# First layer of a two-layer selective-scan network: states in pairs, softplus passes in other slots, old y added at the copy, z copied on VectorE

## The chip, the cores and the metric

One core of a Trainium2 chip runs the whole program. The metric is the device time of one execution in microseconds. Four runs of the kernel before took 11094.7 to 11108.07 us, median 11100.91.

## The reference

Two layers, each with a residual connection, work on x of shape (4, 64, 64, 192). The change touches only the first. In it every image of the batch (4 of them, L = 4096 positions, 192 channels) is normalised and projected to xin and z (384 channels each), and xin is scanned in four directions: by rows, by columns, and both backwards. Cut to what matters:

```python
xz = jnp.einsum('bhwc,ec->bhwe', x, in_proj_weight)
xin, z = jnp.split(xz, 2, axis=-1)
...
delta = jax.nn.softplus(delta + delta_bias[None, :, None])
def step(h, inp):                       # one position of one direction
    dt, ut, bt, ct = inp
    dA = jnp.exp(dt[..., None] * A_k[None])
    dBu = dt[..., None] * bt[:, :, None, :] * ut[..., None]
    h = dA * h + dBu                    # 384 channels x 16 states
    y = jnp.einsum('bkdn,bkn->bkd', h, ct)
    return (h, y)
...
y = out_y[:, 0] + inv_y[:, 0] + wh_y + invwh_y      # the four directions, plus u * D
y = layernorm(y) * jax.nn.silu(z)
return jnp.einsum('bhwd,cd->bhwc', y, out_proj_weight)
```

The sums over the 16 states and over the four directions are what the change is about: y is collected in memory, and each direction adds to what the ones before it have left there.

## The kernel before

`FirstLayer.run` takes the four images one after the other. Between two images, `between` finishes one (normalisation, gate, output projection) and projects the next; then `scans` (L572) does the four directions. Nearly all the time is in `scans`, and within it the order of the work on TensorE, ScalarE, VectorE and GpSimd is the order in which the code issues it (`manual_schedule`); the DMAs all go through SP's queue, in order.

The work of one image is cut into 32 *items*: a direction k (0 to 3) and a chunk c of 512 positions. Items 0 to 15 are directions 0 and 2 (rows, forward and backward), items 16 to 31 directions 1 and 3 (columns), in pairs that run towards each other. An item has 16 *states*, so an image has 512 steps g, and the loop over g is software-pipelined by hand. The 384 channels are three groups d of 128. For state n of an item the engines do the following:

- ScalarE, `b_product` two steps ahead (L716): x in turned form, position on partitions, as delta times u times B of this state, four pieces of 128 positions. `decay` one step ahead (L728): a = exp(A delta), three groups.
- TensorE, `turn_x` one step ahead (L733): transposes of x back to channels on partitions, into PSUM, three buffers, four transposes for each d.
- VectorE, `scan` (L741): the recurrence, one instruction for each d; then a reduce (L751) that copies the last column of h, the `carry` for the next chunk of this direction.
- GpSimd, `c_product` (L755): h times C, in place, after the reduce. Here it is called a product, and c4 is that of state 4.
- TensorE, `add_y` (L768): transposes of h that accumulate in three PSUM banks yp, three steps later (`LAG = 3`); states 0 and 1 are added together at step 4, once the banks are free again.

h is held in seven buffers of one state each (`p7`), a in three, C (`bct`, loaded for two states at once at even steps) in three.

Ahead of the states, `start_y` (L762) puts the old y of the chunk into the banks by an identity matmul, at steps 3 and 4. `load("yold")` gets it from memory: at step 5 of the item before, or, where the direction changes between rows and columns, only after the last item has stored its part (`end_y` at step 3). `end_y` (L781) copies the three banks to SBUF at steps 2 and 3 of the next item, on VectorE, and stores them.

Around this, `Item.steps` (L685) spreads the preparation of the following items over the steps: a tuple (ahead, n, engine, f) runs f at state n of the item that lies `ahead` items before. Delta is a softplus built of passes: dt rows by a matmul (`dt_rows`, L632), `absolute` and `exp` on ScalarE, `plus` (L645) and `minus` (L649) on GpSimd two items ahead, `log` on ScalarE, `rest` (L655) and `total` (L658) on GpSimd one item ahead at states 1 and 4, the dt rows once more, and `delta` (L661) on VectorE at states 7 to 9. `turn` (L675) and `times_u` (L681) follow at states 10 to 13. At each step GpSimd takes the product of the state first and then what `prepare(g, "pool")` has for it.

The gate z is made during items 0 to 8: `gate_in` (L519 by way of `in_proj`) into PSUM at states 13 to 15, `gate_out` (L794) on ScalarE two steps later. The dt rows, the turns of dt, turn_b and the gate share two PSUM buffers (`psm`).

Of the kernel before, what the change touches and what calls it, by code (L numbers as in the profile page):

```python
# [402 lines left out]
class FirstLayer:  # L403
# [168 lines left out]
    def scans(self):  # L572
        nc, tc = self.tc.nc, self.tc
        with ExitStack() as ctx:
            pool = lambda name, bufs, **k: ctx.enter_context(tc.tile_pool(name=name, bufs=bufs, **k))
            p1, p2, p3, p7 = pool("b1", 1), pool("b2", 2), pool("b3", 3), pool("b7", 7)
# [27 lines left out]
            class Item:  # L604
# [80 lines left out]
                def steps(self):  # L685
# [6 lines left out]
                    r += [(2, 15, "pool", self.minus), (1, 2, "act", self.log)]  # L692
                    r += [(1, 1, "pool", self.rest), (1, 4, "pool", self.total)]
# [16 lines left out]
            carry, xTs, xs, as_, hs, cs = {}, {}, {}, {}, {}, {}  # L710
# [26 lines left out]
            def scan(g, d):  # L737
                it, n = flat[g]
                if d == 0:
                    hs[g] = p7.tile([128, ND, LC], F32, name="h")  # L740
# [4 lines left out]
                    0.0 if it.first else carry[it.k, n][:, d : d + 1],  # L745
# [3 lines left out]
                if d == ND - 1:  # L749
                    kept = carry[it.k, n] = pk.tile([128, ND], F32, name=f"carry{it.k // 2}_{n}")  # L750
                    nc.vector.tensor_reduce(kept, last(hs[g], it.k), mybir.AxisListType.X, ALU.max)  # L751
# [5 lines left out]
            def start_y(it, b):  # L757

                if b == 0:
                    it.yp = [ps_y.tile([128, LC], F32, name=f"yp{i}") for i in range(ND)]  # L760
                yo = it.yold.rearrange("p j e -> p (j e)")[:, b * LC : (b + 1) * LC]
                nc.tensor.matmul(it.yp[b], ident, yo, start=True, stop=False, skip_group_check=True)  # L762

            def add_y(g, b):
                it, n = flat[g]
                for i in range(NJ):
# [5 lines left out]
                        start=False,  # L772
# [5 lines left out]
            def end_y(it, b):  # L778
                if b == 0:
                    it.yt = p1.tile([128, NJ, DI], F32, name="yt")  # L780
                nc.vector.tensor_copy(it.yt.rearrange("p j e -> p (j e)")[:, b * LC : (b + 1) * LC], it.yp[b])  # L781
# [9 lines left out]
            def gate_out(t, e):  # L791
                if e == 0:
                    zs[t] = p1.tile([128, ND, LC], F32, name="zg")
                nc.scalar.activation(zs[t][:, e, :], zs.pop((t, e)), AF.Identity, bias=self.bias[:, ND + e : ND + e + 1])  # L794
# [3 lines left out]
            with tc.manual_schedule(engines={nc.tensor.engine, nc.scalar.engine, nc.vector.engine, nc.gpsimd.engine}):  # L798
# [8 lines left out]
                for t in range(NCH):  # L807
                    for e in range(ND):
                        plan.setdefault(t * NS + 13 + e, []).append(("pe", lambda t=t, e=e: gate_in(t, e)))
                        plan.setdefault(t * NS + 15 + e, []).append(("act", lambda t=t, e=e: gate_out(t, e)))  # L810
# [6 lines left out]
                items[0].yold = load("yold", self.y_dram, items[0].k, items[0].c)  # L817
# [8 lines left out]
                for g in range(N + LAG + 1):  # L826
# [11 lines left out]
                    if it is not None:  # L838
# [794 lines left out]
```

## Time and profile before

| | us | share of span |
|---|---|---|
| median of four runs | 11100.91 | |
| the profiled execution | 11094.67 | |
| its span | 11092.5 | 100% |
| scans of image 0, first scan to last | 184.5 to 2377.0 | |
| from the last scan of an image to the first of the next | some 230 | |
| an item in mid-run, first scan to first scan | some 68 | |
| item 16 (rows to columns) | some 86 | |
| VectorE busy | 9690.0 | 87% |
| ScalarE busy | 9776.6 | 88% |
| TensorE busy (matmul) | 9542.3 | 86% |
| GpSimd busy | 8588.4 | 77% |

The granted TensorE clock was 0.939 over the span. A line of groups names the source line, engine, operation, tiles and shape with its count, then busy time, mean nanoseconds of one, and the idle time of the engine in front of it with what ended it. A line of the timeline gives start, length, engine, line, operation, tiles and how many were merged, and in brackets the idle time before it. TensorE's weight loads (PEld) are listed apart from its matmuls. Other groups that the text speaks of:

```
L728 ACT ACTIVATE a<-dt,A_log_f 128x512 f32<-128x512 f32 x6144 | 3978.1, 716 | 0.0
L762 PE MATMUL yp<-yold,ident 128*128 128x512 f32 x768 | 440.6, 658 | 71.5 <-DMA yold<-y 71.5
L661 DVE SCALAR_TENSOR_TENSOR dt<-dp,e 128x512 f32<-128x512 f32 x384 | 255.4, 666 | 65.1 <-POOL e L658 58.5
L781 DVE COPY yt<-yp 128x512 f32<-128x512 f32 x384 | 258.3, 674 | 17.7 <-PE yp L768 17.4 <-issue 0.3
L794 ACT ACTIVATE zg<-zp,bias 128x512 f32<-128x512 f32 x96 | 65.3, 681 | 5.1 <-PE zp L519 5.1
```

### The profile page before, as it was taken

The page shows a single profiled execution, that of the slowest core. Times are in us where ns is not written, and L with a number is a line of the kernel's source. Part 1 is how long each engine was busy: PE and PEld are TensorE (multiplying, and loading weights), DVE is VectorE, ACT ScalarE, POOL GpSimd, SP SyncE. Part 2 cuts the span into 40 slices and gives each one's busy share as a digit, 9 for nine tenths or more (in the row PEclk, how much of TensorE's full clock was granted, in tenths as well). Part 3 has the DMA queues.
Part 4 walks back from the last instruction along what each step waited for, and adds up shares of the span by engine and source line. Part 5 has one row for each costly group of instructions (what it writes and reads, how often), then busy time and mean ns, then how long its engine had stood idle before and what let it go on. Part 6 is the DMA issues. An engine that isn't in the chain of part 4 may idle for free. (4 is left out here: it accounts for less than half of the span.)

```text
span 11092.5 us, 172135 instructions
## 1 busy us (share of the span) xinstructions
PE 9542.3 (86%) x61449; PEld 7262.8 (65%) x61449; DVE 9690.0 (87%) x11515; ACT 9776.6 (88%) x16979; POOL 8588.4 (77%) x2776
## 2 busy tenths in 40 slices
PE   7998888888998888888988888889988888788677
PEld 4776666666776666656766666657766666655366
DVE  4999899976999899968999899949998999878675
ACT  5999999977999999969999999959999999856477
POOL 3999899956999899938999899929998999700270
PEclk8999999998999999998999999989999999989688
DMA  4343344444343344443433444454333434433458
GB/s 125 111 110 99 91 102 98 99 141 126 108 107 99 93 100 98 99 161 109 110 103 95 98 99 97 95 169 109 109 97 96 98 99 98 119 117 122 158 130 275
DMA packets 833672, 1267.54 MB, mean 114 GB/s; under 512 B 102027, under 2 KB 517656, under 8 KB 832293
## 3 DMA queue, kind: packets, MB, share of 16 engines
q1 hardware_dynamic: 827940, 1250.15, 41.5%
q0 software_dynamic: 4864, 6.29, 0.4%
q8 instruction: 488, 8.00, 0.3%
q14 instruction: 380, 3.10, 0.1%
HBM read 955.83 MB, written 300.42 MB: 113 GB/s over the span
## 5 line engine op out<-in xcount | busy, mean ns | idle before, releaser
L755 POOL TENSOR_TENSOR h<-h,bct 128x1536 f32<-128x1536 f32 x2048 | 7065.5, 3473 | 571.9 <-DVE carry L751 471.8
L741 DVE TENSOR_TENSOR_SCAN h<-a,carry,x 128x512 f32<-128x512 f32 x5376 | 6603.2, 1266 | 227.8 <-PE x L733 191.1
L733 PE MATMUL x<-ident,xT 128*128 128x128 f32 x24576 | 3994.3, 286 | 815.3 <-DVE h L741 713.4
L716 ACT ACTIVATE xT<-dtuT,bT 128x384 f32<-128x384 f32 x8192 | 4359.2, 609 | 92.8 <-PE x L733 88.0
L733 PEld LDWEIGHTS x<-ident,xT 128*128 128x128 f32 x24576 | 2797.8, 144 | 2139.4 <-DVE h L741 922.6
L728 ACT ACTIVATE a<-dt,A_log_f 128x512 f32<-128x512 f32 x6144 | 3978.1, 716 | 0.0
L768 PE MATMUL yp<-ident,h 128*128 128x128 f32 x24576 | 3700.9, 277 | 9.2 <-POOL h L755 9.2
L768 PEld LDWEIGHTS yp<-ident,h 128*128 128x128 f32 x24576 | 2942.6, 144 | 78.5 <-issue 62.9
L632 PE MATMUL dp<-xd,w_dtb_f 13*128 13x512 f32 x1536 | 882.8, 657 | 218.5 <-DVE dt L661 214.1
L741 DVE TENSOR_TENSOR_SCAN h<-a,x 128x512 f32<-128x512 f32 x768 | 898.9, 1207 | 190.3 <-PE x L733 114.6
L645 POOL TENSOR_SCALAR wl<-e 128x1536 f32<-128x1536 f32 x128 | 189.6, 1481 | 794.8 <-ACT e L641 404.9
L519 PE MATMUL pp<-xT,w_in 96*128 96x512 f32 x1152 | 537.5, 615 | 1.1 <-DVE xw L562 1.1
L632 PEld LDWEIGHTS dp<-xd,w_dtb_f 13*128 13x128 f32 x1536 | 235.6, 190 | 459.3 <-DVE dt L661 343.4
L762 PE MATMUL yp<-yold,ident 128*128 128x512 f32 x768 | 440.6, 658 | 71.5 <-DMA yold<-y 71.5
L1137 DVE SCALAR_TENSOR_TENSOR acc<-pad,conv_w_s,acc 128x2048 f32<-128x2048 f32 x192 | 439.3, 2342 | 52.4 <-ACT acc L1135 51.8
L638 ACT ACTIVATE e<-dp 128x512 f32<-128x512 f32 x384 | 225.1, 586 | 264.9 <-DVE dt L661 148.9
L1118 POOL MEMSET pad<- 128x66 f32 x12 | 1.9, 160 | 581.8 <-DVE acc L1137 494.3
L658 POOL TENSOR_TENSOR e<-e,wl 128x1536 f32<-128x1536 f32 x128 | 445.5, 3480 | 0.3
L655 POOL TENSOR_TENSOR e<-e,dt 128x1536 f32<-128x1536 f32 x128 | 443.2, 3463 | 0.3
L751 DVE TENSOR_REDUCE carry<-h 128x3 f32<-128x3 f32 x2048 | 322.6, 158 | 70.4
L519 PEld LDWEIGHTS pp<-xT,w_in 96*128 96x128 f32 x1152 | 220.6, 198 | 243.1 <-issue 232.8
L661 DVE SCALAR_TENSOR_TENSOR dt<-dp,e 128x512 f32<-128x512 f32 x384 | 255.4, 666 | 65.1 <-POOL e L658 58.5
(170 smaller groups left out, 6874.5 us busy)
## 6 DMA issues: line engine op xcount, KB each, us to landing
bct<-xp SPq DMA_DIRECT2D x1024, 512.0 KB, 5.1
uT<-uT SPq DMA_DIRECT2D x64, 768.0 KB, 4.7
yold<-y SPq DMA_DIRECT2D x64, 768.0 KB, 7.9
y<-yt SPq DMA_DIRECT2D x64, 768.0 KB, 4.7
uT<-uT SPq DMA_DIRECT2D x128, 384.0 KB, 5.1
yold<-y SPq DMA_DIRECT2D x128, 384.0 KB, 5.5
y<-yt SPq DMA_DIRECT2D x128, 384.0 KB, 4.6
zg<-gate SPq DMA_DIRECT2D x64, 768.0 KB, 6.2
```

The lines of the kernel that those rows point to most:

```text
L519: self.tc.nc.tensor.matmul(pp, self.w_in[:, i, e * 128 : (e + 1) * 128], self.xT[:, i, t * LC : (t + 1) * LC], start=(i == 0), stop=(i == ...
L632: nc.tensor.matmul(self.dp[d], w, self.xd[0 : DR + 1, :], start=True, stop=True)
L655: nc.gpsimd.tensor_tensor(self.e, self.e, self.dt, ALU.subtract)
L658: nc.gpsimd.tensor_tensor(self.e, self.e, self.wl, ALU.add)
L716: nc.scalar.mul(xTs[g][:, j, :], it.dtuT[:, j * DI : (j + 1) * DI], it.bT[:, j, n : n + 1])
L728: nc.scalar.activation(as_[g][:, d, :], it.dt[:, d, :], AF.Exp, scale=scale)
L733: nc.tensor.transpose(xs[g, d][:, j * 128 : (j + 1) * 128], xTs[g][:, j, d * 128 : (d + 1) * 128], ident)
L741: nc.vector.tensor_tensor_scan(along(hs[g][:, d, :], it.k), along(as_[g][:, d, :], it.k), along(xs.pop((g, d)), it.k), 0.0 if it.first els ...
L755: nc.gpsimd.tensor_tensor(hs[g], hs[g], bc(cs[g - n % 2][:, n % 2, :], 1, ND), ALU.mult)
L762: nc.tensor.matmul(it.yp[b], ident, yo, start=True, stop=False, skip_group_check=True)
L768: nc.tensor.matmul(it.yp[b][:, i * 128 : (i + 1) * 128], hs[g][:, d, j * 128 : (j + 1) * 128], ident, start=False, stop=n == NS - 1, is_tr ...
L1137: nc.vector.scalar_tensor_tensor(acc, part(tap), weight(tap), acc, ALU.mult, ALU.add)
```

## The change

Four things in `scans`. h is held in pairs of states (three buffers of two), one reduce serves a pair, the carry is kept by pairs, and the two products of a pair are issued together after the second state. Two of GpSimd's softplus passes change their slot: `minus` from state 15 to 14, `rest` from state 1 to 2, so that at even states, where no product is issued, they stand ahead of the next pair. `start_y` goes: the first add of an item starts the banks, the old y is loaded at step 8 of the item itself, and `end_y` adds it where it copied before. `gate_out` runs on VectorE instead of ScalarE.

```diff
-            p1, p2, p3, p7 = pool("b1", 1), pool("b2", 2), pool("b3", 3), pool("b7", 7)
+            p1, p2, p3 = pool("b1", 1), pool("b2", 2), pool("b3", 3)
...
-                    r += [(2, 15, "pool", self.minus), (1, 2, "act", self.log)]
-                    r += [(1, 1, "pool", self.rest), (1, 4, "pool", self.total)]
+                    r += [(2, 14, "pool", self.minus), (1, 2, "act", self.log)]
+                    r += [(1, 2, "pool", self.rest), (1, 4, "pool", self.total)]
...
-                if d == 0:
-                    hs[g] = p7.tile([128, ND, LC], F32, name="h")
+                if d == 0 and n % 2 == 0:
+                    both[g] = p3.tile([128, 2, ND, LC], F32, name="h")
+                    hs[g], hs[g + 1] = both[g][:, 0], both[g][:, 1]
...
-                    0.0 if it.first else carry[it.k, n][:, d : d + 1],
+                    0.0 if it.first else carry[it.k, n - n % 2][:, n % 2, d : d + 1],
...
-                if d == ND - 1:
-                    kept = carry[it.k, n] = pk.tile([128, ND], F32, name=f"carry{it.k // 2}_{n}")
-                    nc.vector.tensor_reduce(kept, last(hs[g], it.k), mybir.AxisListType.X, ALU.max)
+                if d == ND - 1 and n % 2:
+                    kept = carry[it.k, n - 1] = pk.tile([128, 2, ND], F32, name=f"carry{it.k // 2}_{n}")
+                    nc.vector.tensor_reduce(kept, last(both.pop(g - 1), it.k), mybir.AxisListType.X, ALU.max)
...
-            def start_y(it, b):
-
-                if b == 0:
-                    it.yp = [ps_y.tile([128, LC], F32, name=f"yp{i}") for i in range(ND)]
-                yo = it.yold.rearrange("p j e -> p (j e)")[:, b * LC : (b + 1) * LC]
-                nc.tensor.matmul(it.yp[b], ident, yo, start=True, stop=False, skip_group_check=True)
-
             def add_y(g, b):
                 it, n = flat[g]
+                if n == 0 and b == 0:
+                    it.yp = [ps_y.tile([128, LC], F32, name=f"yp{i}") for i in range(ND)]
...
-                        start=False,
+                        start=n == 0 and i == 0,
...
-                nc.vector.tensor_copy(it.yt.rearrange("p j e -> p (j e)")[:, b * LC : (b + 1) * LC], it.yp[b])
+                part = slice(b * LC, (b + 1) * LC)
+                yt, yo = (t.rearrange("p j e -> p (j e)")[:, part] for t in (it.yt, it.yold))
+                nc.vector.tensor_add(yt, it.yp[b], yo)
...
-                nc.scalar.activation(zs[t][:, e, :], zs.pop((t, e)), AF.Identity, bias=self.bias[:, ND + e : ND + e + 1])
+                nc.vector.tensor_scalar(zs[t][:, e, :], zs.pop((t, e)), self.bias[:, ND + e : ND + e + 1], None, ALU.add)
...
-                items[0].yold = load("yold", self.y_dram, items[0].k, items[0].c)
...
-                            if (n, d) == (LAG, 1) and it is not None and it.yold is None:
-                                it.yold = load("yold", self.y_dram, it.k, it.c)
...
-                        c_product(g)
+                        if n % 2:
+                            c_product(g - 1)
+                            c_product(g)
                         late.append(g)
                         prepare(g, "pool")
-                        if n == 5 and i + 1 < len(items) and items[i + 1].k % 2 == it.k % 2:
-                            q = items[i + 1]
-                            q.yold = load("yold", self.y_dram, q.k, q.c)
+                        if n == 8:
+                            it.yold = load("yold", self.y_dram, it.k, it.c)
```

The order of the adds is unchanged: `late` and `ready` still release a state three steps after its scan.

## The prediction

> **What bounds the kernel now.** I read the page first, then the timelines of VectorE, GpSimd and TensorE over one work item, then the waits, then the change of direction and the end of a batch. "State" n is 0 to 15 within an item; c4 is the product of state 4.
>
> ```profile
> PE 9542.3 (86%) x61449; PEld 7262.8 (65%) x61449; DVE 9690.0 (87%) x11515; ACT 9776.6 (88%) x16979; POOL 8588.4 (77%) x2776
> L755 POOL TENSOR_TENSOR h<-h,bct 128x1536 f32<-128x1536 f32 x2048 | 7065.5, 3473 | 571.9 <-DVE carry L751 471.8
> L741 DVE TENSOR_TENSOR_SCAN h<-a,carry,x 128x512 f32<-128x512 f32 x5376 | 6603.2, 1266 | 227.8 <-PE x L733 191.1
> L751 DVE TENSOR_REDUCE carry<-h 128x3 f32<-128x3 f32 x2048 | 322.6, 158 | 70.4
> ```
>
> Four engines at 77 to 88% over the span are a warning: inside the scans everything is nearly full, so the order of work decides. VectorE is nearest to the bound:
>
> ```profile
> 1004.71 3.62 DVE L741 TENSOR_TENSOR_SCAN h<-a,carry,x 128x512 f32<-128x512 f32 x3
> 1008.37 0.16 DVE L751 TENSOR_REDUCE carry<-h 128x3 f32<-128x3 f32 x1
> 1019.68 0.66 DVE L781 COPY yt<-yp 128x512 f32<-128x512 f32 x1
> 1020.26 1.27 DVE L741 TENSOR_TENSOR_SCAN h<-a,carry,x 128x512 f32<-128x512 f32 x1
> 1047.66 3.62 DVE L741 TENSOR_TENSOR_SCAN h<-a,carry,x 128x512 f32<-128x512 f32 x3 [1.03 <-PE x L733]
> ```
>
> Three scans back to back and their reduce make 3.77 us a state (1004.71 to 1008.48); a copy costs 0.58 (1019.68 to 1020.26). An item takes 68.1 us (mean of the 20 items a batch that I call late: 9 to 15 and 18 to 30). I cut it at two scan starts: A runs from scan (14,0) of the item before to scan (8,1), mean 41.46; B from there to scan (14,0), mean 26.64. In A VectorE hardly idles; the item's 2.1 us of idling lie in B, at states 9 to 11, and end mostly with a turn of x (L733): TensorE stands at a dt row until a PSUM buffer is freed.
>
> GpSimd is late already, in streaks:
>
> ```profile
> 1001.23 3.46 POOL L755 TENSOR_TENSOR h<-h,bct 128x1536 f32<-128x1536 f32 x1 [0.37 <-DVE carry L751]
> 1004.66 1.48 POOL L645 TENSOR_SCALAR wl<-e 128x1536 f32<-128x1536 f32 x1
> 1006.10 3.46 POOL L755 TENSOR_TENSOR h<-h,bct 128x1536 f32<-128x1536 f32 x1
> 1009.53 1.48 POOL L649 TENSOR_SCALAR dt<-wl 128x1536 f32<-128x1536 f32 x1
> 1010.98 6.90 POOL L755 TENSOR_TENSOR h<-h,bct 128x1536 f32<-128x1536 f32 x2
> 1017.82 3.47 POOL L655 TENSOR_TENSOR e<-e,dt 128x1536 f32<-128x1536 f32 x1
> 1021.23 10.34 POOL L755 TENSOR_TENSOR h<-h,bct 128x1536 f32<-128x1536 f32 x3
> 1031.52 3.47 POOL L658 TENSOR_TENSOR e<-e,wl 128x1536 f32<-128x1536 f32 x1
> ```
>
> c4 ends at 1031.52, when state 6 is scanned; its add is due in state 7. Start to start a product takes 3.42, `plus` and `minus` 1.44 each, `rest` and `total` 3.42 each: 18 x 3.42 + 2 x 1.44 = 64.4 us an item, so GpSimd has only 3.7 us to spare.
>
> One large stall stands outside this rhythm, at the change from k = 0, 2 to k = 1, 3, once in each of four batches:
>
> ```profile
> PE yp L762 <- DMA yold<-y: 71.5, 4, 18.2
> 1310.57 2.08 PE L762 MATMUL yp<-yold,ident 128*128 128x512 f32 x2 [17.60 <-DMA yold<-y]
> 1313.61 1.22 DVE L741 TENSOR_TENSOR_SCAN h<-a,x 128x512 f32<-128x512 f32 x1 [17.69 <-PE x L733]
> ```
>
> Item 16 can load its old y only after item 15 has stored; TensorE stands at L762 and VectorE behind it. A of that item is 60.22 us.
>
> **The change, part by part.**
>
> *Old y added at the copy.* The 768 matmuls of L762 (440.6 us busy) go. In ordinary items nothing ends later for them: VectorE doesn't idle at states 3 to 5, so they lie beside scans, and I credit nothing. In item 16 they are what the stall hangs on. The load is now issued at state 8 and needed at state 2 of the next item, over 35 us later; such loads land in 5.5 to 7.9 us. On SP it stands behind one bct load and waits for stores made at state 3: hidden; without that cover it would cost the 17.7 back. The add that replaces the copy reads PSUM and SBUF; the bounds are this copy's 0.67 and the product of the same form at L681, 0.674, so zero. Item 16's A falls from 60.22 to the 42.06 derived below: -18.2 x 4 = **-72.6 us**.
>
> *One reduce for two states.* Eight reduces an item go, 0.15 each (3.77 - 3.62). The new one has 6 results for 3; its bounds are 0.16 and the 64-element copy L627's 0.21; I take 0.16. VectorE loses 5 x 0.15 = 0.75 in A (41.46 to 40.71), and three reduces in B, where the turn of x hides about half: -0.25.
>
> *Products in pairs, passes ahead.* c12 now waits for state 13's reduce, and the GpSimd queue from there is c12, c13, plus, minus, c14, c15, c0, c1, rest, c2, c3, total, c4. GpSimd never catches up inside it: every pair's states are done before its turn. (Its slack sits later: after c7 the pair (8, 9) is met about on time, and (12, 13) with some 2 us idle before it.) From scan (14,0): first product at +0.28 (at 1000.84 the reduce starts, at 1000.95 the next scan, at 1001.23 the product); 8 products x 3.42 = 27.36; plus and minus 2.88; rest and total 6.83; c4 itself 3.47. c4 ends at +40.82. The order of adds is unchanged (three states later), so in state 7 TensorE's queue has the add of c4 between two turns of x for state 8; behind it stand the turn that scan (8,1) needs and the dt rows. The hand-over is priced by
>
> ```profile
> 1035.83 0.47 PEld L768 LDWEIGHTS yp<-ident,h 128*128 128x128 f32 x4
> 1036.26 0.47 PEld L733 LDWEIGHTS x<-ident,xT 128*128 128x128 f32 x4
> ```
>
> 0.05 from a product's end to a waiting add, 0.43 for one add, 0.76 from a turn's first matmul to its scan (medians in the trace): scan (8,1) starts no earlier than 40.82 + 1.24 = **42.06**. VectorE alone would be there at 40.71, so 1.35 us of wait eats the 0.75 saved and 0.6 more. The adds before it hold: c2 ends at +30.5, while its last harmless moment is +31.5 (scan (6,0) at 31.5); c15 ends at +16.8, before the first end_y at 18.5; `total` ends at +37.4, and delta wants it at 37.55. The six pair slots hold too: pair (10, 11) needs the add of c5, about 4 us earlier.
>
> A late item: A +0.6, B -0.25, together +0.35; 80 of them: **+28 us**.
>
> *z on VectorE.* Items 2 to 8 gain three copies, 0.58 by L781's steps (bounds 0.58 and ScalarE's 0.68 at L794), 1.8 in all, in A. There the waits that ScalarE's copies cause today go: 0.49 at state 1, 0.19 at state 3, 0.17 at state 0. A: 42.56 - 0.75 + 1.8 - 0.85 = 42.76, over the chain's 42.06, so GpSimd is hidden. With B's -0.25 nothing but -0.05; I round to -0.1: 28 items, **-3 us**. [...]
>
> *Odd items.* Items 0, 1, 17 and 31 keep the savings without the wait, or nearly (31 has no softplus passes in its A; 1 loses ScalarE waits): 3 us a batch, **-12 us**.
>
> *The tail.* After the last scan two products follow instead of one:
>
> ```profile
> 2377.41 3.42 POOL L755 TENSOR_TENSOR h<-h,bct 128x1536 f32<-128x1536 f32 x1 [0.25 <-DVE carry L751]
> 2380.88 1.53 PE L768 MATMUL yp<-ident,h 128*128 128x128 f32 x12 [2.14 <-POOL h L755]
> ```
>
> The store of y and the next stage's loads queue behind them: +3.42 x 4 = **+14 us**.
>
> Sum: -72.6 + 28 - 3 - 12 + 14 = -46. The profiled execution took 11094.67 us (span 11092.5, 2.2 around it), so 11049; the median of the runs is 6.2 higher, 11100.91, and against it -46 gives **11055 us**, 0.4% faster.
>
> **Rivals.** *The late products cost nothing* (0.17). If TensorE has more lead at state 7 than I think, late items take A 40.71: -1.0 each instead of +0.35, 108 us less: 10947. For it: today's waits of adds for products total only some 25 us. Against it: that is at c4 ending 6 us earlier than it will.
>
> *TensorE leaves state 7 behind and stays so* (0.21), the slower side. The idling at states 9 to 11 comes from TensorE standing at dt rows between turns; after a late c4 it issues two dt rows (1.12 each) and four adds back to back, and each dt row needs a buffer that VectorE frees. By my count B's first gap grows 0.18; if it grows at two or three of these states by half a dt row each, B is +1.2 instead of -0.25: 1.45 x 80 = 116, so 11171. It decides against the change from B +0.35 on (0.6 x 80 = 48). For it: VectorE's idling is there already; against it: c5 and c6 are ready when their turns come, by 1.4 us and more.
>
> *The stall at item 16 only moves* (0.07): the later load or the stores before it wait on SP for bct buffers that late products hold. Then 72.6 comes back: 11128, hardly a change. Against it: 35 us of room.
>
> **How the numbers follow.** The forecast has 0.55. Its own uncertainty is 0.5 us on the late items' sum, 40 us: 11015 to 11095. About 0.2% (22 us) is what a measurement of this kernel can tell. Faster by more than that: 0.17 + 0.43 of the forecast's 0.55 = 0.60. Within: 0.10 of the forecast, 0.03 each of the second and third rival: 0.16. Slower: 0.18, 0.04 and 0.02 from the forecast's edge: 0.24. The range of 8 in 10 takes the first rival to 10945 and most of the second, to 11150.
>
> **What would show it.** Item 16's A near 42, no wait for yold. Late items: A 42.0 to 42.2 with a wait of about 1.3 us of scan (8,1) for x, and behind it TensorE waiting for c4 at L768's successor; GpSimd unbroken from c12 to c7; B 26.2 to 26.6. In items 2 to 8 no such wait. The prediction is wrong if late items' A is near 40.7, if B passes 27, or if adds earlier than c4 hold TensorE.

## The result, and the profile after

The changed kernel takes 11113.51 us (median of 40 runs, 11093.08 to 11140.94) against 11102.99 for the kernel before (60 runs on the same chips). The ratio is 1.0009, 95% interval 1.0005 to 1.0014: a tenth of a per cent slower, where 0.4% faster was predicted. The profiled execution took 11136.58 us (span 11134.7) and lies at the upper end of its own runs, so the traces differ by 42 us where the medians differ by 10.5.

The page after: busy times and groups, in the columns explained above (`scan` has moved to L742, the turn of x is still L733, the reduce is L752, the product L756, the add L764, the copy L779).

```profile
PE 9413.3 (85%) x60681; PEld 7388.5 (66%) x60681; DVE 9589.7 (86%) x10587; ACT 9719.6 (87%) x16883; POOL 8574.7 (77%) x2776
...
L756 POOL TENSOR_TENSOR h<-h,bct 128x1536 f32<-128x1536 f32 x2048 | 7040.6, 3470 | 604.6 <-DVE carry L752 525.0
L742 DVE TENSOR_TENSOR_SCAN h<-a,carry,x 128x512 f32<-128x512 f32 x5376 | 6584.1, 1265 | 431.2 <-PE x L733 342.7
...
L764 PE MATMUL yp<-ident,h 128*128 128x128 f32 x24576 | 3852.9, 285 | 267.6 <-POOL h L756 267.2
...
L779 DVE TENSOR_TENSOR yt<-yp,yold 128x512 f32<-128x512 f32 x384 | 255.5, 666 | 33.0 <-PE yp L764 33.0
```

VectorE has 100 us less to do (9690.0 to 9589.7), as meant, and its scans wait 431.2 us instead of 227.8. The adds of TensorE now wait 267 us for products. The add that takes the copy's place costs 666 ns, the copy cost 674. One number on no line of this view matters most: the granted TensorE clock fell from 0.939 to 0.914 over the span. It runs from 0.914 to 0.919 in the runs of the changed kernel; the eight at 0.915 or below have a median of 11130.6 us, the nine at 0.918 or above 11100.9. So the scatter of this kernel goes with its clock.

By place, in the two profiled executions (late and early items, A and B as in the prediction; early are items 2 to 8):

| | before | after | change in all | predicted |
|---|---|---|---|---|
| late items: A | 41.46 | 42.24 | | 42.06 |
| late items: B | 26.64 | 26.62 | | -0.25 |
| late items, whole (80) | 68.10 | 68.86 | +61 | +28 |
| early items: A | 42.56 | 43.29 | | 42.76 |
| early items: B | 26.49 | 26.78 | | -0.25 |
| early items, whole (28) | 69.05 | 70.07 | +28.5 | -3 |
| item 16 (4) | 86.16 | 69.31 | -67 | -72.6 |
| items 1, 17, 31 (4 each) | | | -7 | -12 |
| between images (3), behind the last | 228.1 | 238.4 | +31, -3 | +14 |
| sum | | | +43 | -46 |

Item 16 did what it should. VectorE's timeline there, image 0 (start, length, engine, line, operation, tiles):

```profile
1308.14 1.22 DVE L742 TENSOR_TENSOR_SCAN h<-a,x 128x512 f32<-128x512 f32 x1 [0.81 <-ACT a L728]
1309.28 0.67 DVE L779 TENSOR_TENSOR yt<-yp,yold 128x512 f32<-128x512 f32 x1
1309.86 1.21 DVE L742 TENSOR_TENSOR_SCAN h<-a,x 128x512 f32<-128x512 f32 x1
...
1312.92 4.55 DVE L742 TENSOR_TENSOR_SCAN h<-a,x 128x512 f32<-128x512 f32 x4
```

Four scans in a row where VectorE stood 17.69 us before; A of item 16 is 42.20 (mean of the four images).

Now a late item (image 0, item 21; state 0 starts at 1644.03, state 3 at 1655.57, state 7 at 1672.14, state 8 at 1676.47). GpSimd's timeline:

```profile
1637.03 6.89 POOL L756 TENSOR_TENSOR h<-h,bct 128x1536 f32<-128x1536 f32 x2 [1.58 <-DVE carry L752]
1643.89 1.46 POOL L645 TENSOR_SCALAR wl<-e 128x1536 f32<-128x1536 f32 x1
1645.44 1.47 POOL L649 TENSOR_SCALAR dt<-wl 128x1536 f32<-128x1536 f32 x1
1646.88 13.73 POOL L756 TENSOR_TENSOR h<-h,bct 128x1536 f32<-128x1536 f32 x4
1660.56 3.47 POOL L655 TENSOR_TENSOR e<-e,dt 128x1536 f32<-128x1536 f32 x1
1663.96 6.92 POOL L756 TENSOR_TENSOR h<-h,bct 128x1536 f32<-128x1536 f32 x2
1670.82 3.50 POOL L658 TENSOR_TENSOR e<-e,wl 128x1536 f32<-128x1536 f32 x1
1674.24 13.69 POOL L756 TENSOR_TENSOR h<-h,bct 128x1536 f32<-128x1536 f32 x4
```

GpSimd is unbroken from c12 to c7, in the order of the prediction. c4 is the first of the last four: it ends near 1677.7, that is 40.9 us after scan (14,0) of the item before (1636.75), where 40.82 was worked out. TensorE's timeline around states 3 and 7:

```profile
1656.98 0.63 PE L733 MATMUL x<-ident,xT 128*128 128x128 f32 x4 [0.76 <-DVE h L742]
1658.75 1.09 PE L733 MATMUL x<-ident,xT 128*128 128x128 f32 x4 [1.14 <-DVE h L742]
1660.52 1.09 PE L733 MATMUL x<-ident,xT 128*128 128x128 f32 x4 [0.68 <-DVE h L742]
...
1664.47 1.06 PE L733 MATMUL x<-ident,xT 128*128 128x128 f32 x4
...
1666.30 0.60 PE L733 MATMUL x<-ident,xT 128*128 128x128 f32 x4
...
1675.19 0.66 PE L733 MATMUL x<-ident,xT 128*128 128x128 f32 x4
1677.77 0.66 PE L764 MATMUL yp<-ident,h 128*128 128x128 f32 x4 [1.92 <-POOL h L756]
...
1679.93 1.06 PE L764 MATMUL yp<-ident,h 128*128 128x128 f32 x4
1680.93 3.78 PE L632 MATMUL dp<-xd,w_dtb_f 13*128 13x512 f32 x4
1684.63 1.12 PE L733 MATMUL x<-ident,xT 128*128 128x128 f32 x4
```

The wait for c4 is there, 1.92 us, as predicted. Two more things were not. In state 3 TensorE has nothing but turns, with idle time between them, since the three matmuls of the old y are gone. In the kernel before they stood there (image 0, item 12, whose states 3 and 4 start at 1016.73 and 1021.68):

```profile
1020.81 0.59 PE L762 MATMUL yp<-yold,ident 128*128 128x512 f32 x1
1021.68 0.63 PE L733 MATMUL x<-ident,xT 128*128 128x128 f32 x4 [0.28 <-DVE h L741]
1022.15 1.02 PE L762 MATMUL yp<-yold,ident 128*128 128x512 f32 x2
1023.01 0.66 PE L733 MATMUL x<-ident,xT 128*128 128x128 f32 x4
```

And in the changed kernel, from 1658.75 to 1665.5, and again from 1679.13, the same four transposes take 1.01 to 1.12 instead of 0.6: the clock is halved. The table by stretches shows it, with PEclk behind the busy times of PE, PEld, VectorE, ScalarE and GpSimd:

```profile
1655.60:1660.50 4.90, 2.34 (x14) 1.53 (x13) 4.87 (x7) 4.90 (x10) 4.90 (x2) 0.82 0.54 88
1660.50:1668.40 7.90, 7.64 (x48) 7.26 (x49) 7.45 (x8) 7.90 (x16) 7.90 (x4) 0.68 0.50 166
1668.40:1676.50 8.10, 7.45 (x51) 5.36 (x49) 7.98 (x10) 8.10 (x16) 8.10 (x3) 1.00 0.53 97
1676.50:1685.90 9.40, 8.13 (x30) 5.26 (x31) 4.34 (x6) 6.53 (x12) 9.40 (x4) 0.64 0.52 128
1685.90:1691.60 5.70, 5.70 (x30) 4.78 (x29) 4.49 (x6) 2.06 (x5) 2.59 (x2) 0.69 0.26 79
```

In state 3 TensorE is busy 2.34 of 4.90 us; the next 8 us are granted 0.68 of full speed. After the wait of state 7 it is the same, and there it hurts, on VectorE:

```profile
1678.97 1.28 DVE L742 TENSOR_TENSOR_SCAN h<-a,carry,x 128x512 f32<-128x512 f32 x1 [1.22 <-PE x L733]
...
1685.86 1.28 DVE L742 TENSOR_TENSOR_SCAN h<-a,carry,x 128x512 f32<-128x512 f32 x1 [3.84 <-PE x L733]
1687.56 1.28 DVE L742 TENSOR_TENSOR_SCAN h<-a,carry,x 128x512 f32<-128x512 f32 x1 [0.43 <-PE x L733]
...
1691.56 3.62 DVE L742 TENSOR_TENSOR_SCAN h<-a,carry,x 128x512 f32<-128x512 f32 x3 [0.75 <-PE x L733]
```

The 1.22 of scan (8,1) is the wait the prediction spoke of. In front of scan (9,0) two dt rows and a turn run at half clock: the dt rows take 3.78 us, where one took 1.12 at full clock (at 1674.14), and the turn 1.12 instead of 0.66. By these numbers about 2 of the 3.84 us are the clock, an estimate; the rest is that both dt rows stand ahead of that turn.

### The profile page after: what moved, and what is told of

It is laid out like the page before. It is cut to its first block, busy times and chain, and to the rows that moved or that the text cites. A ratio compares the mean times of both kernels' runs of the same rounds, so it can differ in the third digit from the quotient of the medians.

```text
span 11134.7 us, 168361 instructions
## 1 busy us (share of the span) xinstructions
PE 9413.3 (85%) x60681; PEld 7388.5 (66%) x60681; DVE 9589.7 (86%) x10587; ACT 9719.6 (87%) x16883; POOL 8574.7 (77%) x2776
## 5 line engine op out<-in xcount | busy, mean ns | idle before, releaser
L756 POOL TENSOR_TENSOR h<-h,bct 128x1536 f32<-128x1536 f32 x2048 | 7040.6, 3470 | 604.6 <-DVE carry L752 525.0
L742 DVE TENSOR_TENSOR_SCAN h<-a,carry,x 128x512 f32<-128x512 f32 x5376 | 6584.1, 1265 | 431.2 <-PE x L733 342.7
L733 PE MATMUL x<-ident,xT 128*128 128x128 f32 x24576 | 4110.4, 293 | 846.6 <-DVE h L742 765.5
L733 PEld LDWEIGHTS x<-ident,xT 128*128 128x128 f32 x24576 | 2922.2, 149 | 1936.9 <-issue 769.0
L764 PE MATMUL yp<-ident,h 128*128 128x128 f32 x24576 | 3852.9, 285 | 267.6 <-POOL h L756 267.2
L764 PEld LDWEIGHTS yp<-ident,h 128*128 128x128 f32 x24576 | 3062.7, 149 | 338.2 <-POOL h L756 338.1
L742 DVE TENSOR_TENSOR_SCAN h<-a,x 128x512 f32<-128x512 f32 x768 | 894.9, 1205 | 136.8 <-ACT a L728 70.5
L934 PE MATMUL op<-w_out,v 128*128 128x192 f32 x1536 | 295.0, 343 | 11.5 <-DVE v L924 9.4
L779 DVE TENSOR_TENSOR yt<-yp,yold 128x512 f32<-128x512 f32 x384 | 255.5, 666 | 33.0 <-PE yp L764 33.0
```

What stands on the lines that cost most here:

```text
L733: nc.tensor.transpose(xs[g, d][:, j * 128 : (j + 1) * 128], xTs[g][:, j, d * 128 : (d + 1) * 128], ident)
L742: nc.vector.tensor_tensor_scan(along(hs[g][:, d, :], it.k), along(as_[g][:, d, :], it.k), along(xs.pop((g, d)), it.k), 0.0 if it.first els ...
L756: nc.gpsimd.tensor_tensor(hs[g], hs[g], bc(cs[g - n % 2][:, n % 2, :], 1, ND), ALU.mult)
L764: nc.tensor.matmul(it.yp[b][:, i * 128 : (i + 1) * 128], hs[g][:, d, j * 128 : (j + 1) * 128], ident, start=n == 0 and i == 0, stop=n == N ...
L934: nc.tensor.matmul(op, v[:, d, j * 128 : (j + 1) * 128], w_out[:, d, :], start=(d == 0), stop=(d == ND - 1))
```

## How the clock is granted, from these traces

In both traces the granted clock is full or half, and changes on a grid of 3.41 us. From the first scan of image 0 to the last of image 3 the kernel before had 232 half windows, the changed kernel 406. A full window that was followed by a half one had a matmul busy share of 0.70 (median of 137 such windows, kernel before) or 0.39 (205, changed kernel); in the item above the two were at 0.46 and 0.44. Where the next was full too, the share was 0.94 and 0.93. The shares overlap: a twentieth of the full windows that were followed by full ones were busy for less than 0.66 (before) or 0.69 (after). Half windows went back to full where the share was high (0.99 or more in 132 of 138 before and in 178 of 206 after, 0.79 at the least), but such a share was not always enough: in the item above TensorE was busy throughout two half windows in a row, from 1679.18 on, and the next was half again. Counting half windows inside A and B of each item shows what goes with one (a window belongs to the stretch in which its middle lies):

| half windows in B | late items before | after | with pairs alone (experiment 6) |
|---|---|---|---|
| 0 | 17 items, B 25.42 | 43, 25.41 | 23, 25.60 |
| 1 | 63, 26.97 | 23, 27.23 | 10, 27.20 |
| 2 | | 2, 28.86 | 7, 28.16 |
| 3 | | 12, 29.44 | 40, 29.38 |

B goes with the number of half windows, nearly alike in three kernels. The table alone doesn't say which of the two is the cause, since a stall also leaves TensorE quiet; experiments 8, 11 and 13 add work to TensorE and leave the rest as it was. In early items A goes the same way: 21 of the 28 had no half window before (A 42.29) and 7 had one (43.36); after, none had none, 11 had one (42.57) and 17 two (43.76). In late items after, A is 42.26 with one and 42.23 with two: there GpSimd's queue sets it and the half clock lies beside.

No long pause stands in front of the half windows of the item above: in its states 3 and 7 TensorE has no gap longer than 1.92 us.

## The experiments

Ratios are against the kernel before on the same chip, with 95% intervals. The numbering has no 7.

**1. The old y at the copy, alone.** The kernel before with `start_y` gone, the load at step 8 and the add in `end_y`; states single, z on ScalarE.

> The kernel before with one part of the change: no identity matmuls of the old y, which is loaded at state 8 and added at the copy. Theory C (clock): TensorE has little to do at state 3 once these matmuls are gone, the granted clock falls to a half for the 3.4 or 6.8 us behind it in most items, and turns and adds of states 4 and 5 hold the scans up: item 16 gives back 67 us, A (scan (14,0) to scan (8,1)) of the other items grows by 0.5 to 1.0, some 50 to 100 us, so 11070 to 11130. Theory G (GpSimd): what was lost at states 4 and 5 came from the late products of the pairs, which aren't here: A stays at 41.4 to 42.5, and the time is 11035 to 11045.

Measured: 11068.83 us, 0.9981 (0.9972 to 0.9990), clock 0.920. Item 16 fell to 66.25 (-19.9 each, -80 in all), but late items rose from 68.26 and 68.01 to 68.71 and 68.53 and early ones from 69.05 to 69.46, +51 us in all, with nothing of the pairs in it. Half windows lie in A of every item (before: 14 of 80 late ones, 7 of 28 early ones).

**8. The same with filler.** Where `start_y` stood, three matmuls of the same shape with no use; the first add starts the bank anew, so nothing of them reaches y.

```diff
+            def start_y(it, b):
+                if b == 0:
+                    it.yp = [ps_y.tile([128, LC], F32, name=f"yp{i}") for i in range(ND)]
+                nc.tensor.matmul(it.yp[b], ident, it.dt[:, b, :], start=True, stop=False, skip_group_check=True)
...
+                        for at, b in (((LAG, 1), 0), ((LAG, 2), 1), ((LAG + 1, 0), 2)):
+                            if at[0] == n:
+                                adds[at[1]].append((start_y, it, b))
```

> Old y at the copy alone, with three identity matmuls an item (on delta, result unused) put back at states 3 and 4. If the clock is what ate most of the 67 us of item 16, A of the late items goes back to 41.4 and of items 2 to 8 to 42.5, and the time is 0.993 to 0.995 of before. Rival (the adds' new start, not the clock, slowed states 4 and 5): 0.998 as without the filler.

Measured: 11028.95 us, 0.9932 (0.9918 to 0.9945), clock 0.944. Groups of the first experiment, then of this one:

```profile
L733 PE MATMUL x<-ident,xT 128*128 128x128 f32 x24576 | 4109.9, 293 | 985.7 <-DVE h L741 884.1
```

```profile
L733 PE MATMUL x<-ident,xT 128*128 128x128 f32 x24576 | 3996.3, 287 | 826.4 <-DVE h L741 724.3
...
L760 PE MATMUL yp<-dt,ident 128*128 128x512 f32 x768 | 428.6, 642 | 0.0
```

With 428.6 us of useless work added, the same turns take 287 ns instead of 293 and the kernel is faster by half a per cent: -73.5 us against the kernel before instead of -24.7. So the removed matmuls had been holding the clock, and taking them away cost 49 of the 73 us that this edit gains with the filler. By place the loss lies in the late items: half windows in A in 80 of 80 without the filler and in 13 with it, state 5 at 4.16 us and 3.86 (3.87 in the kernel before), A at 41.82 and 41.52. The early items don't differ as a whole (69.46 and 69.55). The two intervals don't meet; this pair of runs is the clearest evidence of the study.

**2. The changed kernel with the same filler.**

> The changed kernel with three matmuls an item put back where the old y's stood, of the same form (identity times 512 columns of delta, into the banks that the first add then starts afresh; their result is used by nothing). Theory C: the half clock at state 3 goes in most items, A of items 2 to 8 falls from 43.3 to 42.3 or 42.5, late items keep A 42.2 (GpSimd's chain): 25 to 40 us less than the changed kernel, 11075 to 11090. Theory G: nothing changes, 11105 to 11120, or 1.15 us of TensorE more at three places makes it slower.

Measured: 11156.37 us, 1.0067 (1.0052 to 1.0082), clock 0.934. The early items answer as expected (A 42.34, item 68.51 instead of 70.07; state 5 takes 3.80 us, where it took 4.74 in the changed kernel and 3.91 before); the total, expected at 11075 to 11090, doesn't, since late B goes to 27.86 (items 9 to 15) and 27.07 (18 to 30): 27 late items have three half windows in B, where 12 had. The filler cures the early items; in the late ones the next quiet place, the wait for c4, then decides, and its half windows come oftener. Why oftener isn't settled: the windows run on their own grid of 3.41 us, and what part of the wait falls into one of them depends on how items lie to that grid.

**6. Pairs alone.** The kernel before with the pairs and the two moved passes; the old y by matmul, z on ScalarE.

> The kernel before with the pairs and the moved softplus passes alone; the identity matmuls of the old y stay, and so does the stall at item 16. If the pairs cost what the chain of GpSimd says, late items have A 42.2 (before 41.5), and behind the wait for c4 the granted clock falls to a half at states 8 and 9, so B is 27 to 28 (before 26.6): 1.2 to 2 us an item in 80 items, 100 to 160 us, and 8 to 10 us more between the images: ratio 1.010 to 1.016. Rival: the reduces that are saved pay for the wait, and the loss comes from the other parts: ratio 0.998 to 1.003.

Measured: 11294.99 us, 1.0165 (1.0148 to 1.0181). A of late items 42.27 and 42.32, as in the changed kernel; B 28.20 and 27.76. Its waits (engine, line and tile: total, times, longest):

```profile
PE yp L769 <- POOL h L756: 310.7, 294, 2.4
...
PE yp L763 <- DMA yold<-y: 83.5, 4, 20.9
```

The first row holds all waits of adds for products: by state, 182 us of it are the wait for c4, 104 lie in states 1 and 2 and 20 behind the last scan. The second is the stall of item 16, which the pairs made longer (20.9 against 18.2). Forty of the 80 late items have three half windows in B. Here the pairs cost 193 us; in the changed kernel, by experiment 5, nothing.

**5. The changed kernel without pairs.** Single states, `minus` and `rest` in their old slots.

> The changed kernel without the pairs and with the softplus passes in their old slots: old y at the copy and z on VectorE are left. Old y alone gave a ratio of 0.998. If z on VectorE costs time of itself (three copies of 0.6 in items whose A VectorE bounds, less the ScalarE waits that go: 0.7 to 1.0 us an item, 32 items), the ratio is 1.000 to 1.001. If it costs only beside the pairs, 0.998. The stretch between two images is as before, 225 to 230 us, if the pairs are what lengthened it to 237 to 239.

Measured: 11118.60 us, 1.0013 (1.0004 to 1.0022), before 11102.43. Late items 69.15 and 68.39 (B 27.08 and 26.60), early ones 71.45, the stretch between images 227 to 229. Against the first experiment it has only z on VectorE more, and lies 0.3% higher: the early items take 71.45 instead of 69.46, 56 us in all. So without pairs z is the dear part; with the pairs the early items are back at 70.07, while the stretch between images grows by ten.

**4. The changed kernel with z on ScalarE.**

```diff
-                nc.vector.tensor_scalar(zs[t][:, e, :], zs.pop((t, e)), self.bias[:, ND + e : ND + e + 1], None, ALU.add)
+                nc.scalar.activation(zs[t][:, e, :], zs.pop((t, e)), AF.Identity, bias=self.bias[:, ND + e : ND + e + 1])
```

> The changed kernel with z copied by ScalarE as before. If the move to VectorE is what items 2 to 8 lost, their 70.1 us fall to about 69 and the time by some 28 us, to 11085. If they lost it to the slow clock at states 4 and 5 (theory C), VectorE's 1.8 us less leave A at the later of GpSimd's 42.2 and the slow TensorE: at most 0.5 us an item, 15 us, and ScalarE's waits at state 1 come back: 11095 to 11120.

Measured: 11093.46 us, 1.0000 (0.9991 to 1.0009). Early items 69.30 (A 43.02, B 26.28) instead of 70.07: z on VectorE costs 0.77 an early item (0.27 in A, 0.50 in B), 21 us in all. By the two ratios it is some 10 us, and the intervals overlap (1.0005 to 1.0014 for the changed kernel).

**3. The adds behind the turns.** In the changed kernel the adds of a step come after its three turns instead of between them.

```diff
-                        for f, *a in adds[d]:
+                        for f, *a in sum(adds, []) if d == ND - 1 else []:
```

> The changed kernel with the adds of a step issued behind all three turns of x of that step instead of between them. If the add of c4 holds scan (8,1) because it stands in front of that scan's turn, late items' A falls from 42.2 to about 41 and the wait moves to scan (9,0): 0.3 to 0.7 us an item less, 25 to 55 us, 11060 to 11090. Rival: the wait only moves, B grows by what A loses: 11105 to 11120.

Measured: 11246.24 us, 1.0140 (1.0125 to 1.0154). TensorE waits 22.6 us in all for products, where it was 267.6, and it is much worse all the same: state 5 takes 5.6 to 6.0 us (item 72.0 early, 69.8 and 69.5 late), because the doubled adds of step 4, now in one block, hold the turns of the next state. The adds between the turns are what TensorE does while it waits for VectorE to free a bank of x: without them there its turns wait 1190.4 us for VectorE, where it was 765.5. They can't all go behind.

**9. No pass `rest`.** The changed kernel without `rest`: GpSimd has 3.42 us less ahead of c4, and delta lacks the term that this pass subtracts.

```diff
-                    r += [(1, 2, "pool", self.rest), (1, 4, "pool", self.total)]
+                    r += [(1, 4, "pool", self.total)]
```

> The changed kernel with the pass rest left out (e is not reduced by wl - 1, so delta is wrong): GpSimd's chain from c12 to c4 is 3.4 us shorter. If the wait for c4 and the slow clock behind it are what the pairs cost, A of late items falls to 40.7, no wait for c4 is left, B is 25.6 to 26.5, 1.8 to 2.4 us an item less: 140 to 190 us under the changed kernel, ratio 0.984 to 0.989. Rival: the time is lost elsewhere, in the slow clock at state 3 or on VectorE: ratio 0.998 to 1.001, as the changed kernel's.

Measured: 11026.85 us, 0.9932 (0.9919 to 0.9946). A of late items 41.11 and 41.20: GpSimd's queue did set A, and with the wait for c4 gone 1.1 us an item come back. B didn't fall (27.16 and 26.84, in the changed kernel 26.93 and 26.46), so about half of the expected 140 to 190 us didn't come: the half windows behind state 3 remain (in states 4 and 5), and 75 of 80 late items have one in B.

**10. c4's add one step later.** z on ScalarE and the filler, and the add of state 4 a step later, together with state 5's.

```diff
-                    ready = [x for x in late if x <= g - LAG and
+                    ready = [x for x in late if x <= g - LAG - (x % NS == 4) and
```

> The changed kernel with z on ScalarE, the filler matmuls at states 3 and 4, and the add of state 4 issued one step later, together with that of state 5, so that nothing in front of scan (8,1)'s turn waits for c4; no work is left out. If the wait in that place is the pairs' price, late items' A falls from 42.2 to 40.7 or 41.2, the half clock at state 8 goes, B is 25.6 to 27, and the time is 0.984 to 0.992 of before. Rival: the wait only moves, to c5 in state 8, and the clock falls there: A 40.7 but B 28 or more, 1.000 or above, like the filler with the pairs (1.007).

Measured: 11111.35 us, 1.0013 (1.0003 to 1.0022). A fell to 40.80 in late items, VectorE's own time, so the wait for c4 no longer reaches scan (8,1). But B is 27.50 and 27.25, and 28.71 in early items: a late item as a whole takes 68.14 instead of 68.86, an early one 71.46, where experiment 4, with neither the filler nor the later add, had 69.30. What TensorE waits for is no longer a product (10 us in states 9 and 10 of all late items) but the PSUM buffer of a dt row in state 8, where no add is left to do: 109.5 us in late items and 40.3 in early ones (in that state 70.5 and 24.8 in the kernel before). Item 21 of image 0:

```profile
1674.51 1.12 PE L632 MATMUL dp<-xd,w_dtb_f 13*128 13x512 f32 x2
1677.07 1.12 PE L632 MATMUL dp<-xd,w_dtb_f 13*128 13x512 f32 x2 [1.44 <-DVE dt L661]
...
1678.62 1.73 PE L767 MATMUL yp<-ident,h 128*128 128x128 f32 x8
```

A half window lies in state 9 of 76 late and all 28 early items, on the doubled adds, and scan (10,0) has to wait for a pair slot (54.5 us in all). The rival's total came; that the wait would move to c5 didn't.

**11. Experiment 8 with warm-up matmuls.** A matmul of zeros, 256 columns, added to the item's own first bank ahead of each of the dt rows at states 7 to 9.

```diff
+            def warm():
+                if now:
+                    nc.tensor.matmul(
+                        now[-1].yp[0][:, : LC // 2], ident, zero.to_broadcast([128, LC // 2]), start=False, stop=False, skip_group_check=True
+                    )
...
+                        r += [(2, 7 + d, "pe", warm)]
                         r += [(2, 7 + d, "pe", s(self.dt_rows, d)), (2, 10 + d, "act", s(self.absolute, d))]
```

> Old y at the copy with the filler at states 3 and 4 (0.993), and one more matmul of zeros (256 columns, added to the first bank) ahead of each of the three dt rows at states 7 to 9 that stand waiting for a PSUM buffer. If TensorE's quiet there is what halves the clock at states 9 and 10 (B 25.7 without, 26.3 and 27.4 with such a stretch), B falls to 25.7 or 26 in most items, 0.5 to 0.9 us in 100 items: 0.985 to 0.989. Rival: the matmuls themselves, 0.6 each, stand in front of turns, and B stays or grows: 0.993 to 0.998.

Measured: 10999.40 us, 0.9910 (0.9896 to 0.9923), clock 0.950. The 360 added matmuls were busy for 228.1 us, 0.63 each. No late item has a half window in B (66 of 80 had one in experiment 8), and B is 26.21 and 26.05. It lost nearly all of that in A, 41.93 and 42.04, where a half window at states 3 and 4 has become the rule (78 of 80) in spite of the filler: a late item takes 68.11, in experiment 8 68.17. What was gained lies in the early items, 68.67 instead of 69.55, some 25 us, and the total is short of the expected 0.985 to 0.989. Without pairs and with z on ScalarE, this is the fastest version of the study (its interval overlaps a little with that of experiment 8), faster than both kernels.

**12. No pairs in the last two items.** The changed kernel, where the products of items 30 and 31 are single again and their reduces, whose carry nothing reads, are left out.

> The changed kernel with the products of the last two items of an image issued singly, and their reduces, whose carry nothing reads, left out. From an image's last scan to the next one's first the changed kernel takes 237 to 239, before 225 to 230. If the second product behind the last scan is all of it, this run takes 227 to 231. If, besides, the loads of the next image's input now stand behind the loads of y on SP's queue (here they still do), only the product's 3.4 to 4.5 comes off: 233 to 235.

Measured: 11088.74 us in one run, which says little of the total. The stretch between images is 232.1, 232.4 and 229.6, mean 231.4, against 238.4 and 228.1. So 7.0 of the 10.3 us come from the two late products (by this one run), seen here at the end of image 0: TensorE and then VectorE, before and after.

```profile
2380.88 1.53 PE L768 MATMUL yp<-ident,h 128*128 128x128 f32 x12 [2.14 <-POOL h L755]
```

```profile
2393.05 1.53 PE L764 MATMUL yp<-ident,h 128*128 128x128 f32 x12 [1.11 <-POOL h L756]
2396.91 1.53 PE L764 MATMUL yp<-ident,h 128*128 128x128 f32 x12 [2.33 <-POOL h L756]
```

```profile
2381.58 1.88 DVE L781 COPY yt<-yp 128x512 f32<-128x512 f32 x3 [4.34 <-PE yp L768]
```

```profile
2400.98 1.89 DVE L779 TENSOR_TENSOR yt<-yp,yold 128x512 f32<-128x512 f32 x3 [7.79 <-PE yp L764]
```

The last copies begin 7.8 us after the last reduce instead of 4.3. The 3.3 us left go with a changed order of the loads on SP's queue (two loads of the next image's x were issued ahead of the eight loads of y before, and behind them after and in this run); that it is their cause was not shown.

**13. Warm-up in the wait.** Experiment 2 with the matmuls of experiment 11, and in items 9 to 31 three more in state 7, between the turn and the add that waits for c4.

```diff
+                        if (n, d) == (7, 0) and 8 < i < len(items):
+                            for _ in range(3):
+                                warm()
                         for f, *a in adds[d]:
                             f(*a)
```

> The changed kernel with the filler of the second run, and matmuls of zeros (256 columns each, added to the item's own first bank): one ahead of each of the dt rows at states 7 to 9, and in items 9 to 31 three in state 7 between the turn and the add of c4, where TensorE stands waiting for c4. The wait itself stays. Theory (the clock makes the late products dear: TensorE, quiet while it waits for c4, is granted half clock in states 8 to 10): no half-speed window at states 8 and 9 in late items, B falls from 27.86 and 27.07 to 26.3 or less, the late item from 70.10 and 69.34 to about 68.5; ratio 0.995 to 0.998, against 1.0067 without these matmuls. Rival (TensorE lacks lead, whatever its clock: behind the late c4 it has more to do than time): B stays at 27.4 or above, and with the added matmuls the ratio is 1.006 or more.

Measured: 11153.93 us, 1.0053 (1.0035 to 1.0071), clock 0.950. Waits and groups of experiment 2, then of this one:

```profile
PE yp L767 <- POOL h L756: 312.0, 318, 2.4
```

```profile
PE yp L778 <- POOL h L767: 227.1, 348, 2.3
```

```profile
L744 PE MATMUL x<-ident,xT 128*128 128x128 f32 x24576 | 3927.7, 283 | 664.8 <-DVE h L753 585.3
...
L710 PE MATMUL yp<-zero,ident 128*128 128x256 f32 x1272 | 363.2, 390 | 0.0
```

Both theories got half, and in the total the rival is nearer: 1.0053 against 1.0067, with intervals that overlap. The zeros filled half of the wait for c4 (by state, 183 us of the first row and 91 of the second are this wait), and no item has two or three half windows in B any more (33 of 80 had): 52 have none, 28 one, so the quiet wait does set off the long half-clock stretches. But at no half window B is now 26.62, where it was 25.44 without the zeros: behind a late c4 TensorE has no room for six more matmuls. Late B comes to 27.25 and 26.95, and the price paid in work eats what the clock gave.

## Why the prediction was wrong

**The step that failed first** is the one on the removed matmuls: "they lie beside scans, and I credit nothing". Beside scans they did lie; the cost of taking them away was not time on TensorE's queue but its clock. Experiments 1 and 8 price it where nothing else was changed: 49 us (0.9981 against 0.9932). That the removal with the filler gives -73.5, where -72.6 was worked out for item 16, is in part luck: item 16 alone gave -81 there. The prediction had no rival with the clock in it, though the granted clock of 0.939 was on the page and half windows were there to be counted. In the changed kernel this loss shows in the early items, since GpSimd's queue sets A in the late ones: "-0.1" was forecast and +1.02 came. With the filler (experiment 2) state 5 falls from 4.74 to 3.80 us and an early item from 70.07 to 68.51, 44 us in all, and it is then below the 69.0 that was forecast. The filler doesn't make the changed kernel as a whole faster (1.0067), because B of its late items rises by 0.73.

**z on VectorE: priced about right, in the wrong place.** The forecast of 42.76 for A, against the chain's 42.06, holds 0.70 an early item for z; experiment 4 shows 0.77, 21 us, but 0.27 of it in A and 0.50 in B. The copy itself took 731 ns busy, and 0.64 us from its start to the next scan's, where 0.58 was taken. Part of this cost is clock again: with z on VectorE 24 of 28 early items have a half window in B, with z on ScalarE 14. So what the early items lost beyond the forecast, 31 us, isn't z, which was in it: with the filler and z still on VectorE they do better than forecast. The prices of z and of the clock overlap and don't add up.

**A of the late items: right.** 42.06 was forecast from GpSimd's queue and 42.24 measured; the queue, its order and the wait of scan (8,1) are in the trace as described, and experiments 9 and 10, which take the cause away in two ways, bring A to 41.1 and 40.8. The 0.18 more is 14 us over 80 items. The adds ahead of c4 did wait, which was one of the prediction's signs of being wrong: TensorE stood for 0.70 us in state 1 and 0.42 in state 2 of a late item, 90 us in all. Nothing came of it for VectorE, whose states 1 and 2 take 3.87 and 4.45 us, before 3.89 and 4.38.

**B: "-0.25", measured -0.02.** Even in items with no half window B stands at 25.41 against 25.42, so the three reduces saved there don't show at all, 18 us. The mean of B hides a wide spread: more items without a half window than before (43 against 17), and 12 with three.

**The rival "TensorE leaves state 7 behind"** named the right place and the wrong mechanism. It counted dt rows between turns and buffers; in the changed kernel that alone costs nothing, since 43 of 80 late items have the wait and B at 25.4. With the half clock on top B is 29.4. Where the pairs stand alone (experiment 6) this happens in half of the late items, B is +1.4 and +1.2, and the rival's "+1.2" is what came, with a ratio of 1.0165. Only 12 of 80 show it in the changed kernel; why that is, and so why pairs cost 1.65% in one company and nothing in another, is not settled. How items lie to the 3.41 us grid is a possible reason; it wasn't tested by itself.

**Terms that were right or only off in size.** Item 16: A -18.2 forecast, -18.0 measured; no wait for yold is left, though its loads take 8.2 to 8.6 us to land where 5.5 to 7.9 was assumed. The reduce for two states took 163 ns against 0.16, the add at the copy 666 against 674. The rivals "the late products cost nothing" and "the stall only moves" are both out. The tail was mis-sized: +14 forecast, +28 measured (+31 between images, -3 behind the last), since the last adds and copies come later (7.0 us a gap by experiment 12, where one product of 3.42 was counted), and 3.3 us a gap belong to something else.

**The sum** by these terms is +43 for the profiled execution, 89 us above the forecast: 31 in early items, 33 in late ones (14 in A, 18 in B, with rounding), 14 at the ends of images, and 5 each in item 16 and the odd items. The median of the runs is only +10.5: this profiled run lies at the lowest clock of its kernel's runs (0.914) and the table overstates the typical run by some 30 us. Direction and place are the same in both.

## What to carry to other kernels

Before work on TensorE is removed or moved because it is hidden, ask what its busy share will be in each few microseconds afterwards: here the full windows that were followed by half ones had been busy for 0.70 (median, before) and 0.39 (after), and taking hidden matmuls away cost 49 us (experiment 1 against 8). Test it with useless matmuls in the place of the removed ones; if the kernel gets faster with them, as in experiment 8 (0.9932 against 0.9981), leave them in, but only where TensorE has room for them: in the changed kernel the same filler made it slower (1.0067 against 1.0009). And when a producer's order moves a wait to a place where TensorE has nothing else to do, price that wait with the work behind it at half clock, not at the durations seen before: behind the wait for c4 above a turn took 1.12 us, ahead of it 0.66.

## What the runs showed of the hardware that was not expected

- Half clock came behind windows in which TensorE was at work: full windows that were followed by half ones were busy for 0.70 (median, before) and 0.39 (after).
- The clock rose under transposes alone, and held: from 1661.85 to 1670.32 in the late item above TensorE did nothing but turns and adds, which are all transposes. In that stretch the clock went from half to full (four of them took 1.06 us at 1664.47 and 0.60 at 1666.30) and stayed there.
- A kernel with less clock can be faster: experiment 1 ran at 0.920 and took 0.9981 of the time before, experiment 13 at 0.950 and took 1.0053. Half windows cost where TensorE's work holds up the scans (49 us between experiments 1 and 8); in A of the late items after, 42.26 with one and 42.23 with two, no cost shows.
- Late items came out at a whole number of windows of the grid. In experiment 9 late items took 68.27 (items 9 to 15), 20.0 windows of 3.413 us; in the kernel before they took 68.26. That the length is held there by the grid is a reading of these two numbers, not a test.
